# Transformer block on one core: output weights loaded earlier, operand loads placed behind each chunk's, tail products behind masks, weight checks moved into other pairs

## The chip, the core and the metric

The kernel runs on one core of one Trainium2 chip. The metric is the device time of one execution in microseconds. Three executions of the kernel before took 2225.4, 2226.48 and 2229.58 us; the median is 2226.48. The trace comes from one more, profiled execution.

## The reference, cut to what matters

```python
mod = (silu(c) @ wmod).reshape(B, 6, 1, D)          # B = 2 images, D = 1024
sa, ca, ga, sb, cb, gb = ...                        # ga, gb kept at least 0.25 from zero
h = layernorm(x) * (1 + ca) + sa                    # x: 2 x 1024 x 1024
q, k, v = split(clip(h @ Wqkv.T, -8, 8));  q, k = layernorm(q), layernorm(k)
scores = q k^T / sqrt(32) + slope_h * (pos_k - pos_q), causal    # 32 heads of 32
x = x + ga * ((softmax(scores) @ v) @ Wout.T)
h = layernorm(x) * (1 + cb) + sb
g, u = (h @ Wg.T) * ag, (h @ Wu.T) * au             # 2752 features, weights -1, 0, +1
out = x + gb * (((silu(g) * u) @ Wd.T) * ad)
```

## The kernel before, in words

All large products are done in a Strassen-Winograd form: seven half-size products instead of eight (`SEVEN`, L794; in order P1, P2, U2, P5, U3, P53, U6). Each has an operand made of token blocks (A11, A12, S2, S1, S3, S4, A22) and one made of weight blocks (B11, B21, T2, T1, T3, B22, T4). Products accumulate in PSUM banks x and y, and between products an engine must copy or add a bank out before TensorE may go on in it.

The work has four stages.

1. Query, key and value projections of image 0 (0 to about 360 us).
2. Attention (about 360 to 1289 us). `attention` (L1095) goes through 32 groups, (image b, query half qb, chunk k of four heads), each of 4 or 8 units; a unit is a 128-key block: `scores` (TensorE), exponentials (ScalarE), masks on the diagonal (GpSimd, L1155), then two units later `weigh` (TensorE, the product with v; adds of the exponentials on VectorE and GpSimd, L1183). `settle` sums the exponentials. `chunk(i)` (L1104) loads the q, k and v columns of a group (cq, ck, cv), two groups ahead, in two rotating buffers. Beside it runs dense work, interleaved by hand (`together`, L1246): image 1's projections, the output projection of image 0 and half of that of image 1 (`output`, L1366). For each of its 256-token blocks (b, j), `operand` (L1308) loads reciprocal sums (rb) and four blocks of the attention output (aoA), scales them (L1337) on VectorE (A11, A22) and GpSimd (A12, A21), and forms S1 to S4. `masked` keeps a GpSimd instruction behind the last mask while attention runs. The seven blocks of the output weights come from `weights_b` (L817): the first two, B11 and B21, when the function is called, the other five (T2, T1, T3, B22, T4, 1 MB each) one by one from the list `later`, as the first block's products go on (`ahead`, L1390).
3. The tail: the rest of image 1's output projection, then the tokens of the feed-forward part are laid out and split.
4. Feed-forward. `gate_up` (L1791) goes over 2 images x 11 pairs of 256 features. In every pair the seven products (loop index e = 0 to 6) are each done for gate and up, with tokens split in two parts of reduced mantissa. During pair p the raw weights of pair p+1 are loaded into two of four staging buffers (`stage`), and at e = 4 `weight_operands` makes their operands (copies on ScalarE, sums on GpSimd). Eleven times a piece of the down weights is loaded into the other two buffers (`down_load`), and at e = 3 its block differences are made and stored (`down_parts`). The down projection takes the last 286 us (from 1941).

Weights are tested for being small integers: `small_integers` (L1696) copies a staged weight to int8 on ScalarE (L1705) and compares on VectorE (L1706), counting differences. `check_weights` calls it for both halves of a pair, in image 0 during the pair ahead (e = 4 and 5), for pair 1 in its own first two products, for pair 0 in image 1. `in_range` (L1457) tests the reciprocals. If any test fails, a general kernel follows; it does not run here.

Instructions are handed to a scheduler that fixes the order on each engine by its own estimate; `behind(a, b)` makes a come after b. TensorE's order is pinned in most stages. All these loads are issued by SyncE (queue SP) in one order: a load whose buffer is not free holds up those behind it, and a load also waits for the eighth load before it to land. Pools give fixed places in memory; `SPARE` (L1449) is the width of a filler tile that shifts the pools after it.

Of the kernel before, what the change touches and what calls it, by code (L numbers as in the profile page):

```python
# [480 lines left out]
def kernel(  # L481
# [208 lines left out]
        )  # L690

    last_exp = [None]
    last_chunk = [None]
    chain_copy = [None]
    last_mask = [None]
    beside = [False]

    def masked(ins):
        if beside[0]:
            behind(ins, last_mask[0])  # L700
        return ins
# [115 lines left out]
    def weights_b(pool, w, nm, sums, other=None, swap=False, halfway=None, later=None, loaded=None):  # L817

        made = other is None
        order = ("B11", "B21", "T2", "T1", "T3", "B22", "T4") if made else ("B11", "B21", "B12", "B22", "T1", "T2", "T3", "T4")
        bt = {
            q: (other if q == "B12" or q == "B22" and swap else pool[6 - i] if isinstance(pool, list) else pool).tile(
                [P, KC // 2, HALF], FP, tag=f"w{q}", name=f"w{q}_{nm}"
            )
            for i, q in (reversed(list(enumerate(order))) if made else enumerate(order))
        }

        def load(q):  # L830
            if q in BLOCKS:
                kh, n = BLOCKS[q]
                ins = nc.sync.dma_start(
                    bt[q], w[ds(kh * D // 2, D // 2), ds(n * HALF, HALF)].rearrange("(k p) f -> p k f", p=P)
                )
            elif made:
                ins = nc.sync.dma_start(bt[q], sums[:, PARTS[q]])
            if later is not None and last_chunk[0] is not None:
                behind(ins, last_chunk[0])

        for i, q in enumerate(order):
            if later is not None and i > 1:
                later.append(lambda q=q: load(q))
                continue
            load(q)
            if halfway is not None and q == order[0]:
                halfway()
        if loaded is not None:
            loaded()
# [12 lines left out]
        return bt  # L862
# [232 lines left out]
    def attention(pools, adders, banks):  # L1095
# [8 lines left out]
        def chunk(i):  # L1104
            if i < len(GROUPS) and i not in chunks:
                b, qb, k = GROUPS[i]
                while (b, qb) not in ready:
                    yield None
                n = (qb + 1) * QB
                qc = chp.tile([P, QB], FP, tag="cq", name=f"cq_{b}_{i}")  # L1110
                kc = chp.tile([P, S], FP, tag="ck", name=f"ck_{b}_{i}")
                vc = chp.tile([P, NT, P], FP, tag="cv", name=f"cv_{b}_{i}")
                nc.sync.dma_start(qc, qk_dram[b][0][:, k, ds(qb * QB, QB)])
                nc.sync.dma_start(kc[:, 0:n], qk_dram[b][1][:, k, 0:n])
                last_chunk[0] = nc.sync.dma_start(vc[:, 0 : n // P], v_dram[b][:, 0 : n // P, ts(k, P)])
                chunks[b, qb, k] = chunks[i] = (qc, kc, vc)

        def scores(b, qb, k, jb):
            qc, kc, _ = chunks[b, qb, k]
# [41 lines left out]
        def weigh(b, qb, k, jb, ps):  # L1161
# [17 lines left out]
            if jb:  # L1179

                for half in range(2):
                    dst = acc[1][half][:, :, ds(off, n)]
                    adders[b](half, jb).tensor_add(dst, dst, ps[half][:, :, 0:n])  # L1183

        def settle(b, qb, k, ps):

# [24 lines left out]
        def reciprocals(b, qb, n):  # L1211
            flat = "h (c q) -> (h c) q"
            m = n * QB // NR_
            rc = rsp.tile([P, NR_], FP, tag="rc", name=f"rc_{b}_{qb}")[0:m]
            nc.sync.dma_start(rc, sum_dram[b][qb][0:n].rearrange(flat, q=NR_))
            nc.vector.reciprocal(rc, rc)
            nc.vector.tensor_tensor(most[0:m], most[0:m], rc, ALU.max)
            nc.vector.tensor_tensor(least_r[0:m], least_r[0:m], rc, ALU.min)
            nc.sync.dma_start(rec_dram[b][qb][0:n].rearrange(flat, q=NR_), rc)
# [88 lines left out]
    def operand(b, j, ap_):  # L1308
# [6 lines left out]
        for g in range(4):  # L1315
            nc.sync.dma_start(
                rb[ts(g, HD), 0:nk],
                rec_dram[b][qb].rearrange("(k g) q -> g k q", g=4)[g][0:nk, ds(y0, 2 * P)].partition_broadcast(HD),
            )
        if nk < KC:  # L1320
            nc.scalar.copy(rb[:, nk], right["last"][:, ds(y0, 2 * P)])
        a = {
# [8 lines left out]
        for m, kh, q, eng in blocks:  # L1331
            nc.sync.dma_start(a[q], ao_dram[b][qb][:, ds(kh * 4, 4), ds(y0 + m * P, P)])
        yield

        def scaled(q):
            m, kh, eng = next((m, kh, eng) for m, kh, q_, eng in blocks if q_ == q)
            ins = eng.tensor_mul(a[q], a[q], rb[:, ds(kh * 4, 4), ts(m, P)])  # L1337
            if eng is nc.gpsimd:
                masked(ins)

        scaled("A22")
        scaled("A21")
# [23 lines left out]
    def output(b, js, pools, banks, bt, todo, keep, q0=3, after=None):  # L1366
# [9 lines left out]
        for j in js:  # L1376
# [4 lines left out]
            xs = []  # L1381
            for m in range(2):
                xr = tkp[j % 2].tile([P, D], FP, tag="xr", name=f"xr_{b}_{qts[m]}")
                nc.sync.dma_start(xr, x[b, ts(qts[m], P), :])
                xs.append(xr)
            part_t = {}
            step = {}
# [2 lines left out]
            def ahead(e):  # L1390


                while later and 7 - len(later) <= e + 2:
                    later.pop(0)()
                if e == 2 and nxt not in made and not step and (nxt[0], 2 * nxt[1] * P // QB) in settled:
                    step[0], step[1] = operand(*nxt, ap_), e
                    next(step[0])
                elif e > 2 and step and e > step[1]:
                    step[1] = e
                    next(step[0])  # L1400

# [44 lines left out]

    OUT_US = 112.0
    LEAD, DENSE0, DENSE1 = 16.0, 345.0, 161.0
    SPARE = 1920  # L1449

    def halves(half, jb):
        return (nc.vector, nc.gpsimd)[half]
# [240 lines left out]
    low.close()  # L1693
    late_pools.close()

    def small_integers(w, at, pool):  # L1696


        n = w.shape[0]
# [3 lines left out]
        if len(shape) > 1:  # L1703
            j = j.rearrange("p (a b) -> p a b", a=shape[0])
        hold(nc.scalar.copy(j, w), last_copy)  # L1705
        hold(nc.vector.scalar_tensor_tensor(  # L1706
            j, j, 0.0, w, ALU.add, ALU.not_equal, accum_out=count_a[0:n, at : at + 1]
        ))

    def exact(t, at, bank, pool):  # L1710

# [7 lines left out]
    if True:  # L1719
# [10 lines left out]
        with gu:  # L1730
# [19 lines left out]
                hold(nc.scalar.copy(f["A22"], raw["A22"]), last_copy)  # L1750
                return W

            def check_weights(p, st, halves_=(0, 1)):
                n = PAIRS[p][1]
                for kh in halves_:
                    v = st[kh].rearrange("p a k f -> p (a k) f")[:, :, 0 : 2 * n]
                    small_integers(v, 2 * p + kh, jkp)

            assert NPR == 11
            down_at = {  # L1760
                **{(0, p): i for i, p in enumerate((2, 4, 5, 7, 8))},
                **{(1, p): i + 5 for i, p in enumerate((1, 2, 4, 5, 7, 8))},
            }
            OPERANDS = [qa for _, qa, _, _ in SEVEN]
            OTHERS = [qb_ for _, _, qb_, _ in SEVEN]
# [25 lines left out]
            def gate_up(b):  # L1791
                tiles = [hs_tiles[b, i] for i in range(7)]
                here = None
                for p in range(NPR):
                    n = PAIRS[p][1]
                    if p == 1:
                        pinned[0] = True
                    if (b, p) == (0, 2):
                        in_range()
                    if (b, p) == (0, 0):  # L1800
                        operands_of[b, p] = weight_operands(p, staged.pop(0), b)
# [22 lines left out]
                    for e, (c_, qa, qb_, q) in enumerate(SEVEN):  # L1824
# [252 lines left out]
```

## Time and profile before

| what | value |
|---|---|
| profiled execution | 2229.12 us |
| its span, first to last instruction | 2227.4 us |
| mean granted TensorE clock | 0.989 |
| TensorE busy | 2138.0 us (96%) |
| VectorE, ScalarE, GpSimd busy | 1332.3, 942.4, 1095.3 us |
| median of three runs | 2226.48 us |

The execution is 1.7 us longer than its span. Engines in the trace: PE is TensorE, DVE VectorE, ACT ScalarE, POOL GpSimd, SP SyncE (SPq where it issues a DMA). A line of a timeline has start, duration, engine, source line, operation, output tile, input tiles, shape and count; in square brackets stand the idle time of the engine before it and what released it. Tile names are given without numbers: ck and cq are a chunk's keys and queries, av the weighing, wB_o and wT_o output weights, rb the reciprocals, aoA and aoS operands of the output projection, wst and wdst staged weights, junk the int8 copy, gP, uP, gU, uU partial results of gate and up. TensorE's float32 matmuls appear as two or more records. The granted clock is a share of full speed.

In 50 us windows, TensorE is busy for the whole window or nearly so in most; the windows with less are these:

| window, us | TensorE busy of 50 us | granted clock |
|---|---|---|
| 0 to 50 | 33.70 | 1.00 |
| 250 to 300 | 46.20 | 0.93 |
| 900 to 950 | 37.35 | 0.86 |
| 1000 to 1050 | 47.14 | 0.97 |
| 1050 to 1100 | 44.29 | 1.00 |
| 1150 to 1200 | 46.30 | 1.00 |
| 1250 to 1300 | 42.17 | 0.93 |
| 1350 to 1400 | 43.20 | 0.97 |
| 1400 to 1450 | 42.00 | 0.86 |

### The profile page before, as it was taken

The page shows a single profiled execution, that of the slowest core. Times are in us where ns is not written, and L with a number is a line of the kernel's source. Part 1 is how long each engine was busy: PE and PEld are TensorE (multiplying, and loading weights), DVE is VectorE, ACT ScalarE, POOL GpSimd, SP SyncE. Part 2 cuts the span into 40 slices and gives each one's busy share as a digit, 9 for nine tenths or more (in the row PEclk, how much of TensorE's full clock was granted, in tenths as well). Part 3 has the DMA queues.
Part 4 walks back from the last instruction along what each step waited for, and adds up shares of the span by engine and source line. Part 5 has one row for each costly group of instructions (what it writes and reads, how often), then busy time and mean ns, then how long its engine had stood idle before and what let it go on. Part 6 is the DMA issues. An engine that isn't in the chain of part 4 may idle for free. (4 is left out here: it accounts for less than half of the span.)

```text
span 2227.4 us, 27226 instructions
## 1 busy us (share of the span) xinstructions
PE 2138.0 (96%) x9537; PEld 1169.8 (53%) x9537; DVE 1332.3 (60%) x1811; ACT 942.4 (42%) x1783; POOL 1095.3 (49%) x775
## 2 busy tenths in 40 slices
PE   7999999999999999799999998899999999999998
PEld 2444443333333333232222245688878888788887
DVE  5864652455566643356667678688977555544545
ACT  1322223445444444456556516454554434333331
POOL 2231202443344464576777675678967777313212
PEclk9999999999999999899999999899999999999999
DMA  9888776545425531855544377657768867698765
GB/s 364 306 326 313 267 264 250 190 137 197 170 81 189 165 139 48 272 162 168 152 119 123 113 207 249 216 187 245 246 228 263 262 202 237 225 379 314 271 226 188
DMA packets 319349, 482.44 MB, mean 217 GB/s; under 512 B 16092, under 2 KB 235036, under 8 KB 310244
## 3 DMA queue, kind: packets, MB, share of 16 engines
q1 hardware_dynamic: 317040, 473.24, 63.1%
q10 hardware_dynamic: 2164, 7.38, 0.9%
q8 instruction: 77, 1.26, 0.2%
q14 instruction: 68, 0.56, 0.1%
HBM read 323.01 MB, written 157.55 MB: 216 GB/s over the span
## 5 line engine op out<-in xcount | busy, mean ns | idle before, releaser
L1151 ACT ACTIVATE p<-sc,kw 128x128 f32<-128x128 f32 (+3 forms) x1024 | 422.9, 515 | 388.2 <-PE sc L762 371.1
L1183 POOL TENSOR_TENSOR p<-p,p 128x1024 f32<-128x1024 f32 (+3 forms) x128 | 265.0, 2070 | 214.9 <-PE av L762 190.7
L762 PE MATMUL bank<-wT,a 128*128 128x512 f32 x744 | 351.6, 607 | 2.5 <-DVE raw L1038 1.6
L1183 DVE TENSOR_TENSOR p<-p,p 128x1024 f32<-128x1024 f32 (+3 forms) x192 | 241.1, 1271 | 137.3 <-POOL p L1155 85.3
L762 PE MATMUL bank<-wB,a 128*128 128x512 f32 x552 | 259.2, 605 | 0.0
L762 PEld LDWEIGHTS bank<-wT,a 128*128 128x128 f32 x744 | 132.1, 190 | 186.9 <-issue 169.9
L1155 POOL TENSOR_SCALAR_AFFINE_SELECT p<-p 128x256 f32<-128x256 f32 x256 | 135.4, 542 | 180.6 <-ACT p L1151 169.8
L762 PE MATMUL sc<-cq,ck 32*128 32x512 f32 (+3 forms) x1536 | 181.7, 538 | 15.8 <-DMA ck<-qk 11.2
L762 PE MATMUL av<-p,cv 128*32 128x512 f32 (+3 forms) x1536 | 168.7, 498 | 15.6 <-POOL p L1155 15.5
L762 PEld LDWEIGHTS bank<-wB,a 128*128 128x128 f32 x552 | 97.7, 189 | 134.6 <-issue 126.4
L1957 DVE TENSOR_TENSOR lo<-lo,hi 128x1408 fp32r<-128x1408 f32 x56 | 98.4, 1760 | 89.0 <-ACT hi L1956 88.9
L762 PEld LDWEIGHTS sc<-cq,ck 32*128 32x128 f32 x1536 | 61.8, 184 | 153.1 <-issue 86.1
L1956 ACT CAST hi<-lo 128x1408 fp32r<-128x1408 f32 x56 | 76.9, 1375 | 140.2 <-DMA lo<-act 91.9
L2021 POOL TENSOR_TENSOR early_P<-early_P,x1in 128x512 f32<-128x512 f32 x16 | 35.9, 2246 | 163.9 <-DVE early_P L2019 159.1
L1038 DVE TENSOR_TENSOR raw<-P,bank 128x512 f32<-128x512 f32 x48 | 32.8, 683 | 133.5 <-PE bank L762 100.8
L762 PEld LDWEIGHTS av<-p,cv 128*32 128x32 f32 x1536 | 33.9, 108 | 149.3 <-issue 81.3
L1744 POOL TENSOR_TENSOR wS<-wst,wst 128x1024 fp32r<-128x1024 f32 (+1 forms) x22 | 64.9, 2949 | 91.9 <-PE uy L762 68.8
L762 PE MATMUL uy<-hs,wS 128*128 128x512 f32 (+1 forms) x352 | 90.1, 399 | 5.8 <-DVE uP L1871 5.8
L762 PE MATMUL gy<-hs,wS 128*128 128x512 f32 (+1 forms) x352 | 89.3, 396 | 3.6 <-DVE gP L1871 3.6
L762 PE MATMUL gx<-hs,wA 128*128 128x512 f32 (+1 forms) x352 | 89.3, 396 | 2.4 <-DVE hs L1665 2.4
L762 PE MATMUL gx<-hs,wS 128*128 128x512 f32 (+1 forms) x352 | 88.7, 393 | 1.2 <-DVE hs L1665 1.0
L762 PE MATMUL ux<-hs,wA 128*128 128x512 f32 (+1 forms) x352 | 87.9, 391 | 0.0
(275 smaller groups left out, 4007.5 us busy)
## 6 DMA issues: line engine op xcount, KB each, us to landing
lo<-act SPq DMA_DIRECT2D x56, 704.0 KB
a<-hop SPq DMA_DIRECT2D x20, 1792.0 KB
wm<-in_L_wmod_dram SPq DMA_DIRECT2D x48, 512.0 KB
act<-aS SPq DMA_DIRECT2D x88, 256.0 KB
wB<-in_L_attn_Wqkv_dram SPq DMA_DIRECT2D x21, 1024.0 KB
wst<-in_L_ffn_Wg_dram SPq DMA_DIRECT2D x40, 512.0 KB
wst<-in_L_ffn_Wu_dram SPq DMA_DIRECT2D x40, 512.0 KB
qk<-qs SPq DMA_DIRECT2D x16, 1024.0 KB
```

The costliest lines, as they stand in the source:

```text
L762: return in_order(nc.tensor.matmul(*args, **kw_))
L1038: ins = nc.vector.tensor_add(dst, part_t[MATE[q]], bank)
L1151: last_exp[0] = nc.scalar.activation(p[:, g, lo:hi], sp[:, g, lo:hi], AF.Exp, bias=kw[:, d, h_ : h_ + 1])
L1155: last_mask[0] = nc.gpsimd.affine_select(out=p[:, :, 0:P], in_=p[:, :, 0:P], pattern=[[0, 2], [1, P]], compare_op=ALU.is_ge, fill=0.0, bas ...
L1183: adders[b](half, jb).tensor_add(dst, dst, ps[half][:, :, 0:n])
L1744: ins = nc.gpsimd.tensor_add(f["S1"], raw["A21"], raw["A22"])
L1956: nc.scalar.copy(hi, lo.bitcast(FP))
L1957: nc.vector.tensor_sub(lo, lo.bitcast(FP), hi.bitcast(FP))
L2021: eng.tensor_add(y, y, x1_of.pop(s))
```

## The change

TensorE's instructions and their order stay as they are. The edits:

- **Output weights.** The first two (B11, B21) are put behind the loads of the thirteenth group (`chunk_loads[12]`) instead of the latest group's. For this the filler tile grows from 1920 to 3008 columns, so that the places of these two weights lie clear of the pools of the projections, and the tile of the reciprocals reuses a constant tile (`sc`). Of the other five, one is also taken from `later` behind every chunk's loads.
- **Operand loads.** rb and the four aoA blocks of a block (b, j) are collected in `deferred` and issued behind a chunk's loads (`flush` in `chunk`), A22 and A21 first, A11 and A12 a step later; `operand` may start from the first product on instead of the third. The x rows (xr) go behind the latest chunk too.
- **Scaling products.** Those of the first block are tied to nothing. In the tail, VectorE's and GpSimd's come behind the last add of the exponentials on that engine, GpSimd's behind the last mask as well.
- **Weight checks.** In image 0, pairs 2, 4, 6, 8 and 10 are checked in their own pair: copies at e = 0 and 1, comparisons at e = 2 and 3. In image 1 the same for pairs 1, 3 and 5; pair 0 has copies at e = 2 and 4 and comparisons at e = 3 and 5; pairs 7 and 9 are checked at e = 5 and 6 of the pair ahead. The down pieces move to pairs 1, 3, 5, 7, 9 of image 0 and 2, 4, 6, 7, 8, 9 of image 1. The range test moves from pair 2 of image 0 to pair 4 of image 1.

```diff
+    last_add = {}
+    chunk_loads = []
+    deferred = []
+
+    def flush():
+        while deferred:
+            deferred.pop(0)()
...
-            if later is not None and last_chunk[0] is not None:
-                behind(ins, last_chunk[0])
+            if later is not None:
+                behind(ins, chunk_loads[12] if q in order[0:2] else last_chunk[0])
...
                 chunks[b, qb, k] = chunks[i] = (qc, kc, vc)
+                chunk_loads.append(last_chunk[0])
+                if later:
+                    later.pop(0)()
+                flush()
...
-                    adders[b](half, jb).tensor_add(dst, dst, ps[half][:, :, 0:n])
+                    eng = adders[b](half, jb)
+                    last_add[eng] = eng.tensor_add(dst, dst, ps[half][:, :, 0:n])
...
-            rc = rsp.tile([P, NR_], FP, tag="rc", name=f"rc_{b}_{qb}")[0:m]
+            rc = sc.rearrange("p k c -> p (k c)")[0:m, 0:NR_]
...
+        def load(*args):
+            ins = nc.sync.dma_start(*args)
+            if beside[0] and (b, j) != (0, 0):
+                behind(ins, last_chunk[0])
+
+        def defer(which):
+            for m, kh, q, eng in blocks:
+                if q in which:
+                    deferred.append(
+                        lambda m=m, kh=kh, q=q: load(a[q], ao_dram[b][qb][:, ds(kh * 4, 4), ds(y0 + m * P, P)])
+                    )
+            if (b, j) == (0, 0) or not beside[0]:
+                flush()
+
+        for g in range(4):
+            deferred.append(lambda g=g: load(
+                rb[ts(g, HD), 0:nk],
+                rec_dram[b][qb].rearrange("(k g) q -> g k q", g=4)[g][0:nk, ds(y0, 2 * P)].partition_broadcast(HD),
+            ))
+        defer(("A22", "A21"))
         yield
+        defer(("A11", "A12"))
+        yield
+        flush()
...
             ins = eng.tensor_mul(a[q], a[q], rb[:, ds(kh * 4, 4), ts(m, P)])
-            if eng is nc.gpsimd:
-                masked(ins)
+            if (b, j) != (0, 0):
+                if not beside[0]:
+                    behind(ins, last_add[eng])
+                if eng is nc.gpsimd:
+                    behind(ins, last_mask[0])
...
-                if e == 2 and nxt not in made and not step and (nxt[0], 2 * nxt[1] * P // QB) in settled:
-                    step[0], step[1] = operand(*nxt, ap_), e
+                if e <= 2 and nxt not in made and not step and (nxt[0], 2 * nxt[1] * P // QB) in settled:
+                    step[0], step[1] = operand(*nxt, ap_), min(e, 1)
...
-    SPARE = 1920
+    SPARE = 3008
...
+            OWN_CHECKS = ((2, 4, 6, 8, 10), (0, 1, 3, 5))
+            AHEAD_CHECKS = ((1, 7), (1, 9))
...
-                **{(0, p): i for i, p in enumerate((2, 4, 5, 7, 8))},
-                **{(1, p): i + 5 for i, p in enumerate((1, 2, 4, 5, 7, 8))},
+                **{(0, p): i for i, p in enumerate((1, 3, 5, 7, 9))},
+                **{(1, p): i + 5 for i, p in enumerate((2, 4, 6, 7, 8, 9))},
...
-                    if (b, p) == (0, 2):
+                    if (b, p) == (1, 4):
                         in_range()
...
-                        if (b, p) == (0, 1) and e < 2:
-                            check_weights(1, here, (e,))
-                        if (b, p) == (1, 0) and e in (4, 5):
-                            check_weights(0, first_staged[0], (e - 4,))
+                        if p in OWN_CHECKS[b]:
+                            mine = here if e == 0 and p else first_staged[0] if e == 0 else mine
+                            for kh, at in enumerate((3, 5) if p == 0 else (2, 3)):
+                                if e == at - 2 + (p == 0):
+                                    rounded[kh] = check_copy(p, mine, kh)
+                                if e == at:
+                                    check_compare(p, mine, kh, rounded.pop(kh))
...
-                            if nb == 0 and np_ > 1:
-                                check_weights(np_, here, (0,))
-                            elif np_ == 0:
+                            if np_ == 0:
                                 first_staged[0] = here
-                        if e == 5 and nb == 0 and np_ > 1:
-                            check_weights(np_, here, (1,))
+                        if e in (5, 6) and (nb, np_) in AHEAD_CHECKS:
+                            rounded[e - 5] = check_copy(np_, here, e - 5)
+                            check_compare(np_, here, e - 5, rounded.pop(e - 5))
```

More of the change, by code (lines that the diff above doesn't have):

```diff
@@ L1314, in operand @@
         nk = KC - 1 if (b, qb, KC - 1) == GROUPS[-1] else KC
[L1315 to L1319, printed above, removed]
         if nk < KC:
@@ L1330, in operand @@
         )
-        for m, kh, q, eng in blocks:
-            nc.sync.dma_start(a[q], ao_dram[b][qb][:, ds(kh * 4, 4), ds(y0 + m * P, P)])
+        def load(*args):
[16 more added lines that the diff above has]
+        defer(("A22", "A21"))
         yield
+        defer(("A11", "A12"))
+        yield
+        flush()
         def scaled(q):
@@ L1383, in output @@
                 xr = tkp[j % 2].tile([P, D], FP, tag="xr", name=f"xr_{b}_{qts[m]}")
-                nc.sync.dma_start(xr, x[b, ts(qts[m], P), :])
+                ins = nc.sync.dma_start(xr, x[b, ts(qts[m], P), :])
+                if beside[0] and last_chunk[0] is not None:
+                    behind(ins, last_chunk[0])
                 xs.append(xr)
@@ L1394, in ahead @@
                     later.pop(0)()
-                if e == 2 and nxt not in made and not step and (nxt[0], 2 * nxt[1] * P // QB) in settled:
-                    step[0], step[1] = operand(*nxt, ap_), e
+                if e <= 2 and nxt not in made and not step and (nxt[0], 2 * nxt[1] * P // QB) in settled:
+                    step[0], step[1] = operand(*nxt, ap_), min(e, 1)
                     next(step[0])
-                elif e > 2 and step and e > step[1]:
+                if e >= 2 and step and e > step[1]:
                     step[1] = e
@@ L1694, with rounded_copy @@
     late_pools.close()
-    def small_integers(w, at, pool):
+    def rounded_copy(w, at, pool):
         n = w.shape[0]
@@ L1705, in small_integers, with differs @@
         hold(nc.scalar.copy(j, w), last_copy)
+        return j
+    def differs(w, j, at):
         hold(nc.vector.scalar_tensor_tensor(
-            j, j, 0.0, w, ALU.add, ALU.not_equal, accum_out=count_a[0:n, at : at + 1]
+            j, j, 0.0, w, ALU.add, ALU.not_equal, accum_out=count_a[0 : w.shape[0], at : at + 1]
         ))
+    def small_integers(w, at, pool):
+        differs(w, rounded_copy(w, at, pool), at)
     def exact(t, at, bank, pool):
@@ L1751, in weight_operands, with check_copy, check_compare @@
                 return W
[L1753 to L1757, printed above, removed]
+            def check_copy(p, st, kh):
+                v = st[kh].rearrange("p a k f -> p (a k) f")[:, :, 0 : 2 * PAIRS[p][1]]
+                return rounded_copy(v, 2 * p + kh, jkp)
+            def check_compare(p, st, kh, j):
+                v = st[kh].rearrange("p a k f -> p (a k) f")[:, :, 0 : 2 * PAIRS[p][1]]
+                differs(v, j, 2 * p + kh)
+            OWN_CHECKS = ((2, 4, 6, 8, 10), (0, 1, 3, 5))
+            AHEAD_CHECKS = ((1, 7), (1, 9))
+            rounded = {}
             assert NPR == 11
             down_at = {
-                **{(0, p): i for i, p in enumerate((2, 4, 5, 7, 8))},
-                **{(1, p): i + 5 for i, p in enumerate((1, 2, 4, 5, 7, 8))},
+                **{(0, p): i for i, p in enumerate((1, 3, 5, 7, 9))},
+                **{(1, p): i + 5 for i, p in enumerate((2, 4, 6, 7, 8, 9))},
             }
```

## The prediction

> **What bounds the kernel now.** I read the page first, then TensorE's list of waits, then the timelines of TensorE, SyncE, VectorE and GpSimd at each long wait.
>
> ```profile
> PE 2138.0 (96%) x9537; PEld 1169.8 (53%) x9537; DVE 1332.3 (60%) x1811; ACT 942.4 (42%) x1783; POOL 1095.3 (49%) x775
> ...
> PEclk9999999999999999899999999899999999999999
> ```
>
> TensorE is busy for 2138.0 of 2227.4 us. The diff leaves its instructions and their order alone, so it can move only the 89 us of idle time and the time run at a reduced clock; PEclk dips at slices 17 and 26. The list of TensorE's waits (columns: us in total, times, longest) names the causes:
>
> ```profile
> PE av L762 <- POOL p L1155: 15.5, 11, 4.8
> PE sc L762 <- DMA ck<-qk: 11.2, 1, 11.2
> ...
> PE uy L762 <- DVE uP L1871: 5.8, 2, 4.4
> ...
> PE gy L762 <- DVE gP L1871: 3.6, 1, 3.6
> ```
>
> The timeline of TensorE shows four long ones, each on an edit of this change:
>
> ```profile
> 942.25 2.09 PE L762 MATMUL sc<-cq,ck 32*128 32x512 f32 x8 [11.22 <-DMA ck<-qk]
> ...
> 1282.61 1.00 PE L762 MATMUL av<-p,cv 128*32 128x128 f32 x8 [4.81 <-POOL p L1155]
> ...
> 1407.79 3.78 PE L762 MATMUL uy<-hs,wS 128*128 128x512 f32 x8 [4.37 <-DVE uP L1871]
> ...
> 1437.66 3.78 PE L762 MATMUL gy<-hs,wS 128*128 128x512 f32 x8 [3.63 <-DVE gP L1871]
> ```
>
> Together 24.0 us of waits. After each the clock is low for some us: eight such matmuls take 1.81 us from start to start in the steady stage, 3.58 behind the last two waits. From 1440 to 1940 us TensorE waits only once for more than 0.25 us (1.42), so checks moved within that stretch have nothing left to win.
>
> **A. The chunk load (wait of 11.22).** SyncE's timeline shows what stood ahead of chunk 19's loads:
>
> ```profile
> 915.65 1.74 SPq L837 DMA_DIRECT2D wT_o<-wt  x2
> 918.58 5.99 SPq L1316 DMA_DIRECT2D rb<-rec  x4
> 925.00 8.97 SPq L1332 DMA_DIRECT2D aoA<-ao  x3
> 934.07 1.84 SPq L1178 DMA_DIRECT2D ao<-aot  x1
> 935.96 0.49 SPq L1113 DMA_DIRECT2D cq<-qk  x1
> 936.50 0.51 SPq L1114 DMA_DIRECT2D ck<-qk  x1
> ```
>
> The buffer was free at 914.75, after the last score of chunk 17, but the queue was held by two 1 MB weights, four reciprocal loads that need 6 us to issue, and operand loads whose issues stretch over 9 us. The DMA engines were full (share 1.0 to 1.16 from 915 to 935).
>
> What the wait costs: 11.22, and in the windows behind it the clock is 0.50 while 2.75 us of work run and 0.63 for 5.0 us: 2.75 x 0.5 + 5.0 x 0.37 = 3.2. Together 14.4.
>
> What is late next: the first two weights leave this place, but in the changed SyncE order the loads of chunk 19 still stand behind two 1 MB weights, four rb loads, two aoA loads (one fewer, and none that waits for an engine) and the ao store of chunk 17. That store follows ScalarE's copy of 925.31 + 0.59 = 925.9. From 910 on, when the v store releases the queue in both kernels, 3.5 MB of transfers (v, gates, x rows, a weight, ao, cv), a second weight, 1 MB of rb at about 200 GB/s (270 and 180 in the slices from 925), 0.5 MB of aoA and a third weight must pass: at 400 GB/s else, 8.8 + 2.5 + 5.2 + 1.3 + 2.5 = 20.3, so until about 930. The chunk's 0.5 MB and the landing take 2 to 4 us more: it lands at 933 to 935, and TensorE is ready at 931.0. An estimated 3 us of wait stay, and 1.4 us of low clock: gain 14.4 - 4.4 = **10.0**, bounds 4 (backlog as before) and 14.4.
>
> One row bears on those 1.4 us: behind a wait of 2.43 us (matmul at 1385.71) seven matmuls take 3.16 us to the next start instead of 1.59, so a short wait here already cost 1.6. The Trainium skill (TensorE: Matmul & The Clock Gate, What's actually happening) puts the clock at half only after an idle window of about 3.4 us. By it the wait of 3 would cost no clock and A would gain 11.4; the row decides for 10.0.
>
> **B. The tail product (4.81).** GpSimd reaches its product of the next operand before the last two masks, and it starts only when rb has landed:
>
> ```profile
> 1280.43 1.76 POOL L1337 TENSOR_TENSOR aoA<-aoA,rb 128x512 f32<-128x512 f32 x1 [3.31 <-issue]
> 1282.15 0.76 POOL L1155 TENSOR_SCALAR_AFFINE_SELECT p<-p 128x256 f32<-128x256 f32 x2
> ```
>
> VectorE's product starts at the same time, 1280.38, so I read the blank release as that landing. In the changed order both engines do the last masks and adds first: masks at 1277.1 to 1277.9, the last weighing at 1277.9, the four sums by 1279.6. Queued behind VectorE's product is the reciprocal (3.36 us), and the transposes wait for it. With rb still landing at 1280.4 the product ends at 1281.1, the reciprocal at 1284.4; the transposes started at 1289.2. Gain **4.8**. Bounds: 3.0 (the new wait of 2.9 us costs 1.8 of clock) and 6.2 (rb early, reciprocal at once).
>
> **C. The weight checks (4.37 and 3.63).** VectorE runs two comparisons of pair 1 ahead of the add that frees TensorE's bank:
>
> ```profile
> 1401.08 2.78 DVE L1706 SCALAR_TENSOR_TENSOR junk<-junk,wst 128x2048 int8<-128x2048 int8 x1
> ...
> 1403.79 3.34 DVE L1706 SCALAR_TENSOR_TENSOR junk<-junk,wst 128x2048 int8<-128x2048 int8 x1
> ...
> 1407.06 0.68 DVE L1871 TENSOR_TENSOR uP<-uP,uy 128x512 f32<-128x512 f32 x1
> ```
>
> Without them the add starts at 1401.1, before the bank is needed at 1403.2. The second wait follows two more comparisons (3.28, 4.48) and four range operations (1.31 + 1.28 + 1.37 + 0.28); all of these leave pairs 1 and 2, and one comparison of wdst (2.3 to 3.4) comes into pair 1 after its fourth product. Low clock: 1.77 + 0.73 behind the first, 1.77 + 1.12 behind the second. Total 8.0 + 5.4 = 13.4.
>
> What is late next: pair 3's weights. Before, their four loads were issued at 1409 to 1411, 44 us ahead of the pair's start at 1455.2. Now pair 1's wdst takes their buffers, and they wait for GpSimd's four differences (6.0 us by 1430.55 to 1436.5), its S4 (2.85) and the stores: S1 starts 1412.8, S3 ends about 1421, differences 1427, S4 1430, two activation sums 1432.5, loads from 1434, landed 6 to 7 us later, at 1440 to 1441 (the loads of 1405.4 to 1407 were there by 1412.8). Pair 3 now starts at 1390.5 + 2 x 25.4 = 1441.3, and needs a 1.05 us copy first: 0 to 2 us late, I take 1.0. ScalarE's queue in pair 1 (copy of wdst, copy of pair 2's weights, 1.9 each, then two copies for TensorE) has about 0.4 us to spare: 0.5. Gain 13.4 - 1.5 = **11.9**, bounds 6 (pair 3 late by 4 us and at low clock) and 13.4.
>
> The ten moved pairs of comparisons cost nothing elsewhere: between the second product's end and the seventh's start lie 14.5 us, and two comparisons at their slowest (4.48), the multiply (0.75) and the adds (2.7) make 12.4. Without GpSimd's contention they take 2.28 each. In image 1, VectorE is busy 27.6 of 50 us from 1750 to 1900. At image 1's pair 0 the splits of tokens fill VectorE (47.5 of 50); the comparison now goes ahead of the last split there, which then ends at 1680.6, 2.0 before its product at 1682.6: 0, with up to 3 us lost if it is late.
>
> **D. Early weights and the other operands.** The two early 1 MB loads pass beside DMA shares of 0.4 to 0.6 at 650 to 800 us, where TensorE waits for no load: 0; if a projection weight were held, 2.5 us each. Operand loads now come behind a chunk's loads: image 0's third block is complete at about 1005, its first product is at 1034; for image 1's second block the loads go out at about 1197 and its GpSimd product stands between masks at 1209. No cost, 3 us of slack; bounds -3 to +3 for the smaller mask waits (15.5 - 4.8 = 10.7), whose GpSimd order hardly changes.
>
> **Sum**: 10.0 + 4.8 + 11.9 = 26.7. The profiled execution took 2229.12 us (span 2227.4 and 1.7 around it), 2.6 above the median of 2226.48, so it becomes 2202.4 and the median **2199.8**, about 2200. About 0.2% (4.5 us) is what a measurement of this kernel can tell from no change.
>
> **Rivals.**
> 1. The chunk still waits: the transfers ahead of it, not the order, decide. For it: the engines were full from 915 to 935 and only 0.25 MB of what stood between 915 and the chunk's load leaves. Against it: the operand loads that waited for GpSimd and TensorE to release their buffers now stand behind the chunk. A gains 4: 2206. The Trainium skill (DMA: Bandwidth & Descriptors, Queues, rings and completion order) has each engine consume a ring's descriptors in order, which is this mechanism; the 5.75 us from the issue of ck to its first use agree.
> 2. The checks' wait returns as a wait for pair 3's weights: C gains 6: about 2206. For it: 44 us of lead become none.
> 3. All waits go whole, and the smaller mask waits shrink by 3: 14.4 + 6.2 + 13.4 + 3 = 37.0: 2189.
> 4. Slower: a GpSimd product beside attention waits for an operand load that now follows the chunk's loads, with masks queued behind it, as at 1280. One such costs 4.8 and 1.8 of clock (0.28 in the weighing, 1.55 in the sums behind it) = 6.6; five operand blocks are loaded this way. The point from which it decides is four of them (26.4); with all five and A at its lower bound, 33.0 - 20.7 = 12.3 us slower: 2239. Against it: the slacks in D.
> 5. No change: three or four such waits, 2226.
>
> **How the numbers follow.** Forecast (2195 to 2204) 0.50, rival 1 0.18, rival 2 0.13, rival 3 0.09, rival 4 0.05, rival 5 0.05. Rivals 1 and 2 together give 2212. The range that leaves out 4, 5 and the far half of 3 is 2190 to 2214. Faster 0.90, same 0.05, slower 0.05.
>
> **What would show it.** A: the wait on ck at 3 us or less, no dip of the clock at 940. B: masks before the product, the last weighing without a wait, and the reciprocal as what the transposes wait for. C: no TensorE wait on uP or gP in pairs 1 and 2; if pair 3 waits for wst copies, rival 2. D: no new POOL wait above 2.7 us between 1000 and 1250. A gain below 15 us would make the sum wrong, a new wait above 5 us its reasons.

## The result and the profile after

The changed kernel took 2217.76 us (median of five runs, 2215.18 to 2219.94) beside 2226.48 for the kernel before: ratio 0.9952, 95% interval 0.994 to 0.9964. Timed once more on another occasion it took 2215.13 beside 2227.68, ratio 0.9937 (0.9923 to 0.995). It is faster by 9 to 13 us. I had forecast 26.7. The profiled execution took 2216.45 us with a span of 2214.7; the span of before was 2227.4.

The page of the changed kernel has the same matmuls and nearly the same busy time, and the two dips of PEclk are gone (a slice is 55 us long, so shorter stretches of low clock do not show in it):

```profile
PE 2133.0 (96%) x9537; PEld 1167.9 (53%) x9537; DVE 1322.8 (60%) x1811; ACT 944.3 (43%) x1783; POOL 1089.4 (49%) x775
...
PEclk9999999999999999999999999999999999999999
```

The list of TensorE's waits (us in total, times, longest) shows that the largest one shrank and did not vanish, that the 4.8 ahead of the last weighing and the 4.4 on uP are gone, and that two others are new or larger (xr was 0.7, ux was not in the list):

```profile
PE av L769 <- POOL p L1166: 10.1, 13, 2.7
...
PE sc L769 <- DMA ck<-qk: 7.0, 1, 7.0
...
PE bank L772 <- DVE xr L750: 3.2, 1, 3.2
PE gy L769 <- DVE gP L1921: 2.3, 1, 2.3
...
PE ux L769 <- ACT uU L1916: 2.2, 1, 2.2
```

**A ledger by matmul.** TensorE runs the same instructions in the same order in both kernels, so the n-th matmul of one trace can be set against the n-th of the other. The difference of their starts is what has been gained up to that point, and where it changes is where time was won or lost. Waits and low clock are both in it.

| matmul | before, us | after, us | ahead by | change since the row above |
|---|---|---|---|---|
| behind the projections' last long wait | 292.75 | 291.78 | 0.97 | |
| first score of chunk 19 | 942.25 | 935.15 | 7.10 | +6.1 |
| last of the low clock behind it | 948.86 | 940.73 | 8.13 | +1.0 |
| a transpose in attention | 1218.69 | 1214.74 | 3.95 | -4.2 |
| first of the last weighing | 1282.61 | 1274.06 | 8.55 | +4.6 |
| first transpose of the tail | 1289.21 | 1280.52 | 8.69 | +0.1 |
| first matmul on the last split in pair 0 | 1385.71 | 1379.55 | 6.16 | -2.5 |
| behind the two waits of the checks | 1443.71 | 1424.04 | 19.67 | +13.5 |
| in pair 3 (index e = 3) | 1468.45 | 1457.94 | 10.51 | -9.2 |
| image 1, pair 0 | 1673.38 | 1660.90 | 12.48 | +2.0 |

From there to the end nothing changes. The 0.97 us of the first row are won in the projections, for which no run gives a cause. Most of the forecast gains are in this column; so are three losses (4.2, 2.5, 9.2) that the forecast put at 0, 0 and 1.5. The timeline of TensorE in the changed kernel shows the waits that make up the rest of chunk 19's and the losses in the tail and the pairs:

```profile
935.15 2.09 PE L769 MATMUL sc<-cq,ck 32*128 32x512 f32 x8 [6.98 <-DMA ck<-qk]
...
1280.52 0.66 PE L772 MATMUL bank<-ident,xr 128*128 128x128 f32 x4 [1.82 <-DVE last L1206]
1313.11 0.66 PE L772 MATMUL bank<-ident,xr 128*128 128x128 f32 x4 [3.15 <-DVE xr L750]
...
1428.69 2.11 PE L769 MATMUL ux<-hs,wS 128*128 128x512 f32 x8 [2.22 <-ACT uU L1916]
1439.20 2.14 PE L769 MATMUL gx<-hs,wA 128*128 128x512 f32 x8 [1.15 <-ACT wA L1784]
1447.64 2.08 PE L769 MATMUL gx<-hs,wS 128*128 128x512 f32 x8 [0.85 <-ACT gP L1916]
1453.86 3.01 PE L769 MATMUL gy<-hs,wS 128*128 128x512 f32 x8 [2.33 <-DVE gP L1921]
```

**Pairs 2 and 3.** GpSimd's timeline at these waits:

```profile
1415.43 1.75 POOL L1829 TENSOR_TENSOR wdsum<-wdst 128x512 f32<-128x512 f32 x1
...
1420.65 1.29 POOL L1832 TENSOR_TENSOR wdsum<-wdst,wdsum 128x512 f32<-128x512 f32 x1
1421.90 4.44 POOL L1791 TENSOR_TENSOR wS<-wst,wS 128x1024 fp32r<-128x1024 f32 x1
1426.31 1.71 POOL L1868 TENSOR_TENSOR aS<-uP,uU 128x512 f32<-128x512 f32 x1
1427.98 3.34 POOL L1868 TENSOR_TENSOR aS<-uU,aS 128x512 f32<-128x512 f32 x1
```

VectorE's comparisons of pair 2 beside them:

```profile
1421.20 2.89 DVE L1744 SCALAR_TENSOR_TENSOR junk<-junk,wst 128x2048 int8<-128x2048 int8 x1
...
1426.82 3.35 DVE L1744 SCALAR_TENSOR_TENSOR junk<-junk,wst 128x2048 int8<-128x2048 int8 x1
```

And ScalarE's timeline, with the two copies that TensorE waits for:

```profile
1428.05 0.58 ACT L1916 COPY uU<-ux 128x512 f32<-128x512 f32 x1 [6.13 <-POOL aS L1868]
1438.10 1.04 ACT L1784 CAST wA<-wst 128x1024 fp32r<-128x1024 f32 x1 [8.49 <-DMA wst<-in_L_ffn_Wu_dram]
```

GpSimd's last weight difference for pair 2 (L1791) stands behind the four differences of the piece of down weights (wdsum, from 1415.43), and it takes 4.44 us beside a comparison of pair 2 that began ahead of it (2.85 without one, below); the activation sums come behind it. ScalarE cannot copy the next uU until the sum that reads the old one is done: TensorE waits 2.22. The stores of the sums stand ahead of pair 3's weights in SyncE's queue, so these go out at 1431.8 and arrive at 1438.1: the pair starts 1.15 late, and its own copies and sums are late too (0.85 and 2.33, and a window at half clock).

### The profile page after: what moved, and what is told of

It reads as the page before. It is cut to its first block, busy times and chain, and to the rows that moved or that the text cites. A ratio compares the mean times of both kernels' runs of the same rounds, so it can differ in the third digit from the quotient of the medians.

```text
span 2214.7 us, 27209 instructions
## 1 busy us (share of the span) xinstructions
PE 2133.0 (96%) x9537; PEld 1167.9 (53%) x9537; DVE 1322.8 (60%) x1811; ACT 944.3 (43%) x1783; POOL 1089.4 (49%) x775
## 5 line engine op out<-in xcount | busy, mean ns | idle before, releaser
L1195 DVE TENSOR_TENSOR p<-p,p 128x1024 f32<-128x1024 f32 (+3 forms) x192 | 246.6, 1300 | 131.3 <-POOL p L1166 75.2
L769 PE MATMUL ux<-hs,wS 128*128 128x512 f32 (+1 forms) x352 | 87.4, 390 | 2.2 <-ACT uU L1916 2.2
```

The lines of the kernel that those rows point to most:

```text
L769: return in_order(nc.tensor.matmul(*args, **kw_))
L1195: last_add[eng] = eng.tensor_add(dst, dst, ps[half][:, :, 0:n])
```

## The experiments

Times are medians beside the kernel before of the same occasion: 2227.35 for checks_only, tail_only, no_defer and piece_later; 2227.82 for weights_only, pair2_unchecked, free_and_prompt and keys_first; 2227.68 for the last two. A ledger comes from one profile of each kernel, so it need not agree with the medians; where nothing else is said it is taken against the first profile of before.

**One part alone, three kernels.** Each is the kernel before with some lines of the change: checks_only those of the weight checks (copies, comparisons, the places of the down pieces and of the range test), tail_only the first five below (and the first block's products tied to nothing, as in the change), weights_only the rest of them, with the wider filler tile and the reused tile that make room.

```diff
+                    last_add[eng] = eng.tensor_add(dst, dst, ps[half][:, :, 0:n])
...
+                if not beside[0]:
+                    behind(ins, last_add[eng])
+                if eng is nc.gpsimd:
+                    behind(ins, last_mask[0])
...
+                behind(ins, chunk_loads[12] if q in order[0:2] else last_chunk[0])
...
+                if later:
+                    later.pop(0)()
```

> The kernel before with the weight-check part of the change alone. Theory 1 (the checks' gain is given back one pair later, by the first piece of down weights that now stands in pair 1): the two waits of 4.4 and 3.6 us and their 5.4 us of low clock go (13.4), new waits in pairs 2 and 3 with their low clock take 9.2, image 1's pair 0 gives 2: a gain of about 6, near 2220. Rival (the new waits arise only because the other parts bring TensorE there earlier): no wait above 1 us between pairs 2 and 3, a gain of 12 to 15, near 2213.

It took 2221.14 us, ratio 0.9973 (0.9963 to 0.9983): 6.2 faster. In its ledger the two waits give 13.6, pairs 2 and 3 take 7.6 (waits of 2.11 and 0.68, one of 2.3 on gP, and low clock), image 1's pair 0 gives 2.1. The new waits come with the checks' new places and need no other part of the change: the rival is out.

> The kernel before with the tail products tied behind the last adds and masks, and nothing else. Theory: the wait of 4.81 us ahead of the last weighing goes and 4.7 us stay with the kernel, minus up to 2.4 that the tail's next block loses (in the changed kernel its layer norm came 2.4 us later): a gain of 2.3 to 4.7, 2222 to 2224. Rival: the loss of 2.4 us in the tail belongs to the operand loads, and the gain is the whole 4.7.

It took 2223.90 us, ratio 0.9983 (0.9974 to 0.9992): 3.4 faster; 4.6 in the ledger at the last weighing. The tail's next transposes wait for xr for 1.06, not 3.15. So the tie of the products gives its whole wait, and the tail's loss belongs to another part (the ledger moves by 0.1 from the tail's first transpose to pair 0).

> The kernel before with the output weights' part alone: the first two loaded behind the thirteenth group, one of the others taken behind every chunk's loads. Theory: this is what brought chunk 19 forward with the operand loads issued at once, 1.3 us at the weighing ahead and 3.4 at the keys: a gain of 4 to 5, near 2222.5. Rival (the deferred operand loads did it): the wait for the keys stays at 11 us, no gain, 2227.

It took 2224.48 us, ratio 0.9985 (0.9977 to 0.9994): 3.3 faster where 4 to 5 were expected, with a wait of 7.7 on chunk 19's keys. The output weights do bring the keys forward, as said: the ledger has 5.6 at the keys and the low clock behind them, of 7.2 in the changed kernel, and gives 2.9 back in attention. The three medians add up to 12.9; the whole change, which has the operand loads besides, gave 8.7 and 12.6.

**Operand loads at once (no_defer).** The changed kernel with the four rb and four aoA loads issued in one go at the third product, as before.

```diff
...
-        defer(("A22", "A21"))
-        yield
-        defer(("A11", "A12"))
-        yield
-        flush()
+        for m, kh, q, eng in blocks:
+            nc.sync.dma_start(a[q], ao_dram[b][qb][:, ds(kh * 4, 4), ds(y0 + m * P, P)])
+        yield
...
```

> The changed kernel with the operand loads (rb and aoA) issued at once, as before, in place of behind a chunk's loads; all else as changed. Theory 2 (the deferred loads make VectorE's and GpSimd's scaling products late, with masks and layer-norm copies queued behind them: 3.8 us lost at 1055 to 1066 and 3.7 at 1213 to 1219): these losses go, so 7.5 faster, less what chunk 19's keys lose by standing behind operand loads again, up to 3: 2210 to 2213. Rival (those losses come because TensorE arrives there earlier, whatever the loads do): they stay, and with chunk 19 later the time is 2218 to 2221.

It took 2213.33 us, ratio 0.9943 (0.993 to 0.9956). The number came out at the upper end of the range (0.3 above it) and the reason only in part. The tail's loss is gone, which is theory 2 in the tail: TensorE's timeline there reads

```profile
1311.29 0.66 PE L772 MATMUL bank<-ident,xr 128*128 128x128 f32 x4 [0.26 <-DVE xr L750]
```

In attention the two losses that I had named are gone too (no wait of 2 us at the layer-norm transposes of 1055 and 1214), but so are the gains next to them: a mask wait of 1.46 us that the deferred loads had removed at 1194.80 is back with 2.11. Waits and low clock over the matmuls of the ledger's row that lost 4.2 us (948.86 to 1218.69 in before), summed from the traces:

| kernel | waits, us | low clock, us |
|---|---|---|
| before, two profiles | 15.0; 16.5 | 1.7; 0 |
| checks_only, tail_only (attention as before) | 15.0; 14.7 | 3.0; 3.1 |
| changed, two profiles | 16.9; 15.2 | 3.2; 1.7 |
| no_defer | 15.3 | 4.7 |

(A low window is counted at half of the time that TensorE worked in it.) The waits lie between 14.7 and 16.9 whatever the loads do. Theory 2 fails for attention: of the 4.2 us of the ledger, 1.8 are waits and 1.5 low clock, the rest is not placed, and the second profile of the changed kernel loses only 0.4 over the same matmuls. In the tail the deferred order does cost: the waits at its layer norm are 3.8 and 3.0 in the changed kernel, 3.8 and 4.4 in piece_later and pair2_unchecked, which have that order, 0 to 2.2 in those without. Over the whole tail, from its first transpose to the last split in pair 0, the ledgers of these four profiles lose 2.5, 6.6, 3.7 and 6.7 us; those without that order lose 2.1 at most (the second profile of before; 1.0 otherwise).

**The piece of down weights out of pair 1 (piece_later).**

```diff
-            OWN_CHECKS = ((2, 4, 6, 8, 10), (0, 1, 3, 5))
-            AHEAD_CHECKS = ((1, 7), (1, 9))
+            OWN_CHECKS = ((4, 6, 8, 10), (0, 1, 3, 5))
+            AHEAD_CHECKS = ((1, 2), (1, 7), (1, 9))
...
-                **{(0, p): i for i, p in enumerate((1, 3, 5, 7, 9))},
+                **{(0, p): i for i, p in enumerate((2, 3, 5, 7, 9))},
```

> The changed kernel with the first piece of down weights moved from pair 1 to pair 2 of image 0, and the check of pair 2 moved to pair 1 of image 1. Theory 1: pair 1 has room again, pair 3's weights are loaded a pair ahead, and the 9.2 us lost in pairs 2 and 3 (waits of 2.2, 1.15, 0.85 and 2.3 and low clock) go: near 2209. Rival: the same lateness appears one pair later, at pair 4, whose weights now wait for pair 2's piece: waits of 2 to 5 us there, near 2215.

It took 2210.01 us, ratio 0.9922 (0.9907 to 0.9938). From 1390 us to the end of image 0 TensorE does not wait for more than 0.25 us once. GpSimd's timeline has the same difference in 2.85 us:

```profile
1417.66 2.85 POOL L1791 TENSOR_TENSOR wS<-wst,wS 128x1024 fp32r<-128x1024 f32 x1
```

SyncE issues pair 3's weights from 1403.2, a pair ahead. Pair 4 does not wait either. Theory 1 holds, for the piece and pair 2's check together.

**Which of the two (pair2_unchecked).** The same edit of the checks; the piece stays in pair 1.

> The changed kernel with only the check of pair 2 moved to pair 1 of image 1; the first piece of down weights stays in pair 1. It splits theory 1. If the piece alone makes pair 3's weights late (its differences and stores hold the staging buffers), waits of 1 us or more at pair 3's start and behind it stay, 5 us or more of the 9.2, near 2213 or above. If the comparisons of pair 2 do it (they slow GpSimd's sums beside them and hold VectorE), the waits go, near 2209.

It took 2215.11 us, ratio 0.9946 (0.993 to 0.9963), which by its time speaks for the piece; but from pair 2 on only one wait of over 0.25 us is left, the 2.33 on gP, and pair 3's start is in time. Both have a part. The 2.33 is the piece's: in all five profiles with the piece in pair 1 (checks_only, no_defer, pair2_unchecked and two of the changed kernel), GpSimd's differences for pair 3 begin 1.2 to 2.0 us after that pair, and TensorE waits 2.3 on gP; in the other seven they begin 8 to 11 us ahead of it and the wait is not there. For the rest the split is not sharp, since the wait of 2.22 also was absent in the second profile of the changed kernel.

**Both mended (free_and_prompt).** The edits of no_defer and of piece_later together.

> Both mended together: operand loads issued at once, and the first piece of down weights in pair 2 with pair 2's check in image 1. Theories 1 and 2 speak of different stages, so their gains add: 9.2 in the pairs and 4 in attention and the tail below the changed kernel, near 2204. Rival (the two share a cause, such as TensorE arriving early): less than the sum, 2207 to 2210.

It took 2205.38 us, ratio 0.99 (0.9883 to 0.9917), near the sum: 22.4 faster. Its profile is the fastest of its four runs, so its ledger ends 26.7 ahead of before; that this is the forecast's number is chance, for the wait on chunk 19's keys is still 7.21.

**The place of chunk 19's keys (keys_first).** free_and_prompt, with `keys`, a part of `chunk` that takes the tiles cq and ck and loads them, called for chunk 19 two units earlier:

```diff
                 queue.append((*u, scores(*u)))
+                at = GROUPS.index(u[0:3]) + 2
+                if u[3] == 4 * u[1] + 3 and at in (19,):
+                    ahead_keys[at] = keys(at)
```

> The kernel free_and_prompt with the query and key loads of chunk 19 issued right behind the last scores of chunk 17, ahead of one 1 MB weight, four rb loads, three operand loads and an ao store; the values keep their place. Theory 3 (what delays the keys is their place in SyncE's queue): issued at 914 to 916, they land before 924, TensorE does not wait at chunk 19; the 9.0 us of wait and about 2 of low clock go, near 2193. Rival (the transfers themselves are the limit: the DMA engines are full from 910 to 935): the keys land later than 928 all the same, or the wait moves to the values, the weight or the operands behind them, 4 to 8 us, near 2200.

It took 2195.38 us, ratio 0.9853 (0.9833 to 0.9872): 32 faster than before, 10.0 faster than free_and_prompt, the fastest of all. SyncE's timeline (ck at 929.36 in free_and_prompt):

```profile
916.64 0.48 SPq L1119 DMA_DIRECT2D ck<-qk  x1
917.30 0.32 SPq L844 DMA_DIRECT2D wT_o<-wt  x1
920.02 4.31 SPq L1339 DMA_DIRECT2D rb<-rec  x4
924.43 5.34 SPq L1355 DMA_DIRECT2D aoA<-ao  x3
```

TensorE's first score of chunk 19:

```profile
930.47 1.14 PE L769 MATMUL sc<-cq,ck 32*128 32x512 f32 x8
```

No wait stands behind that score, and none came behind it on the values, the weight or the operands: the next is 0.40, on chunk 20's keys. The same transfers run, in another order. For the changed kernel SyncE's timeline has the keys behind all of them:

```profile
911.43 4.23 SPq L1340 DMA_DIRECT2D rb<-rec  x4
917.25 1.96 SPq L1340 DMA_DIRECT2D aoA<-ao  x2
919.31 4.01 SPq L1214 DMA_DIRECT2D sum<-rs  x1
923.72 0.34 SPq L844 DMA_DIRECT2D wT_o<-wt  x1
...
926.89 0.32 SPq L1121 DMA_DIRECT2D ck<-qk  x1
```

**What varies by itself (before_again, after_again).** Both kernels unchanged.

> The kernel before, unchanged, profiled once more. Theory 4 (the low clock is given in windows of 3.41 us on a grid that has another phase in every execution, so a wait of 1.5 to 2.7 us costs 1.7 us more or nothing by chance): the waits between 1021 and 1219 us repeat within 0.5 us of the first profile's 13.2, but the low clock there is no longer nought: 1.7 to 4.7 us, as in the kernels tail_only and checks_only, whose attention is the same. Rival (the clock follows from the order of the work): nought again.

One run took 2227.91. The waits between 1021 and 1219 us are 14.6, 1.4 more than in the first profile, and the low clock there is nought again: the expectation failed. It was formed on the wrong stretch: the one wait of over 2 us there fell across two windows in both profiles of before (see below), and a window at half clock that the first profile did have, at 1016.9, lies just ahead of it. What did vary is the wait on chunk 19's keys: 8.1 us, where the first profile had 11.2 (checks_only and tail_only 11.2 and 11.6).

> The changed kernel once more, timed and profiled. Theory 4: each wait repeats within 0.5 us (6.98 on chunk 19's keys, 3.15 in the tail, 2.22, 1.15, 0.85 and 2.33 in pairs 2 and 3), the low clock beside the short ones does not; the median stays 7 to 11 us below the kernel before. Rival (the waits themselves vary from run to run): one of them moves by over 1 us.

The waits on the keys (7.8), in the tail (3.0) and in pair 3 (1.01, 0.87, 2.29) repeat within 0.9 us; the 2.22 on uU is absent and a wait on split tokens at pair 0 is 3.7 instead of 2.5. So single waits of 1 to 3 us do come and go from run to run. The ledger of this second profile has +6.7 at the keys with the low clock behind them, -0.4 in attention, +4.6 at the last weighing, -6.6 in the tail, +13.9 behind the checks' waits, -6.6 in pairs 2 and 3 and +2.1 at image 1's pair 0, and the same end (12.6).

## Why the prediction was wrong

Most mechanisms were those forecast and the direction was right; the sum was 14 to 18 us too large. Step by step:

- **A, forecast 10.0, measured 7.2 in the ledger.** The step that failed is "TensorE is ready at 931.0". The keys came at 935.15, the end of the forecast's 933 to 935. But 931.0 was read from the trace of before, in which TensorE had lost 1.43 us at 917, ahead of the same spot. That wait went, 1.0 us had been won in the projections besides, and TensorE was ready at 928.2; since the landing hangs on SyncE's queue, the time won ahead of it came back as wait: 6.98 in place of 3. So the ledger's 7.2 are 4.2 of the wait, 1.0 of low clock and 1.9 won at 917. The size also depends on the run: the old order waited 11.2 in the first profile, in checks_only and (11.6) in tail_only, but 8.1 in the second profile of before, and between the second profiles of both kernels A gives 3.9. Rival 1 foresaw a wait that stays, because the transfers and not the order decide. keys_first speaks against that reason: issued 10 us earlier than in the changed kernel, the same keys are there in time with all the other transfers still running, so their place in the queue decides.
- **B, forecast 4.8, measured 4.7.** Right, with the reciprocal as what the transposes then wait for (1.82 on "last"). Alone: 3.4 by medians.
- **C, forecast 11.9, measured 6.3** (13.5 - 9.2 + 2.0; 9.4 in the second profile: 13.9 - 6.6 + 2.1). The gross term, 13.4, was right to 0.1 us. The failed step is "0 to 2 us late, I take 1.0". It was right for pair 3's start (1.15; loads at 1431.8, forecast 1434) and left out what late weights bring behind the start: the pair's copies and sums are late too (0.85 and 2.33, the latter also where the start was in time), ahead of it a sum on GpSimd held a buffer that ScalarE needed (2.22), and there was low clock. The "about 0.4 us to spare" were counted for ScalarE's queue in pair 1; in pair 2 it stood still for 6.13 us until that buffer was free. Rival 2 was this mechanism, and I gave it 0.13; that its price (a gain of 6) is so near the 6.3 is partly luck, as the 2.0 of image 1's pair 0 are in the 6.3 and not in the rival. The gain of 2.0 at image 1's pair 0, where I had put 0 to -3, is mostly the wait of 1.42 on uP that went with the comparisons' new places there (checks_only has it too; that move was not tried alone).
- **D, forecast 0, measured -2.5 in the tail** (-6.6 in the second profile) and nothing that can be told from chance in attention. The slack of 3 us was reckoned for attention; it named no operand of the tail, where no_defer shows that the deferred order costs. The bound of -3 held in the first profile alone. Rival 4's mechanism (products late, masks behind them) did happen twice, but each had a gain beside it of about the same size.
- **Low clock.** The 1.4 us that A paid for a wait of 3 and the 5.4 that C won were each read from one trace, and chance has a part in them (last section): behind the two waits of the checks the clock was low for 6.83 us each in both profiles of before and in tail_only, for 3.41 each in weights_only. In attention the changed kernel's profiles lost 3.2 and 1.7 to it, those of before 1.7 and nothing.

A failed because time that is won ahead of a transfer which is bound to a queue comes back as a wait for that transfer. In C the same holds for the 1.15 us of pair 3's start; the rest came from engines that the late weights, the piece's differences and the comparisons crowded. Rivals 1 and 2 rest on different stages and can both come true; here the waits that they foresaw came, and the 2212 that the prediction gives for the two together, a gain of 14.8, is near the 12.7 us by which the two spans differ.

## What to carry to other kernels

When the order on the bounding engine is fixed, compare two kernels instruction by instruction: the gain so far shows each loss where it happens, and a loss can be undone by itself, as here, where three small edits made 10 us into 32. When a wait is removed, move the whole engine forward before asking what is late next: loads that hang on a queue do not move with it. And a load that the next work needs belongs ahead of those with slack in its queue, at the moment its buffer is free.

## What the runs showed of the hardware

**The clock is decided in windows of 3.41 us.** In the clock records of all twelve profiles (they begin 15 to 18 us after the first instruction), every stretch at half clock (but the one that the kernel's end cuts off) lasts 3.41, 6.83, 10.24 or 13.65 us, and within a profile all start on one grid of 3.413 us, whose phase differs from run to run. TensorE's idle time within one window tells what the next one gets: with 2.0 us or more of idle the next was at half clock in all of 80 windows, with 1.8 to 2.0 in 16 of 23, with 1.5 to 1.8 in 4 of 34. With less idle time no window at full clock was followed by one at half clock (7478 windows); but one already at half clock was followed by another in 9 of 9 cases with 0.8 to 1.5 us of idle, in 5 of 79 with less. So the same wait costs some us more or nothing, as it falls into one window or across two. The same matmul in before_again and in tail_only, with the same wait:

```profile
1088.30 1.20 PE L762 MATMUL av<-p,cv 128*32 128x384 f32 x8 [2.67 <-POOL p L1155]
1089.42 1.13 PE L762 MATMUL bank<-wB_o,aoA 128*128 128x512 f32 x2
```

```profile
1091.63 1.85 PE L763 MATMUL av<-p,cv 128*32 128x384 f32 x8 [2.66 <-POOL p L1156]
1093.41 2.08 PE L763 MATMUL bank<-wB_o,aoA 128*128 128x512 f32 x2
```

In the first the idle time fell 1.47 and 1.20 us into two windows, and the clock stayed; in the second 1.97 us fell into one, and the next two windows were at half clock. Behind this wait, 2.7 us long in all twelve profiles, the ledger loses 2.7 us in tail_only and checks_only, 2.6 in no_defer, 1.3 in the first profile of the changed kernel and nothing in its second or in before. The Trainium skill (TensorE: Matmul & The Clock Gate, What's actually happening) says that the window is free-running and 3413 ns long; the traces agree. It puts the half clock behind an idle window of that length; here 2.0 us of idle within one were enough.

**GpSimd and VectorE wait for each other.** GpSimd's difference of 128x1024 took 2.40 us in pair2_unchecked and 2.85 in piece_later, and 4.44 beside VectorE's comparison of 128x2048 in the changed kernel. VectorE's sums of 128x512 took 0.69 us with GpSimd idle (at 1462.78 in before), 1.67 and 1.60 beside GpSimd's differences of 128x512 (pair 1 of the changed kernel), and 2.76 and 2.71 beside those of 128x1024 (pair 2). The times fit an order in which the one that comes second does nothing until the first is done: the difference of 4.44 us overlaps the end of the comparison for 2.19 and needs 2.25 more; the sum of 2.76 overlaps a difference for 2.21 and needs 0.55 more. What counts is which begins first: a difference of 2.85 us in before (at 1422.08) has a comparison beside it for 2.33 of them, but one that began behind it. VectorE's adds out of a PSUM bank are not held: that of 1413.13 in the changed kernel took 0.68 us in the middle of a difference.
